# Alternating the order in which an FFN's float32r matmuls read their moving columns

## The chip, the cores and the metric

The kernel runs on one core of one Trainium2 chip. The metric is the device time of one execution in microseconds. Times are medians of several executions, and a profiled execution has a time of its own.

## What is computed

The input `x` has 4 x 1024 tokens of 512 features, all in float32. Two layers follow, each with a normalised input and a normalised output that is added to the residual:

```python
x = x + _layernorm(_L0_attn_ref(_layernorm(x), Wq, Wv, Wo, Wg, ln_gamma, ln_beta, beta))
x = x + _layernorm(_L0_ffn_ref(_layernorm(x), gate_w, up_w, down_w, gate_scale, up_scale, down_scale))
```

The first layer is a retention: `v = x @ Wv.T` is run through a decaying scan along the tokens, multiplied by `q = x @ Wq.T`, normalised, gated with `silu(x @ Wg.T)` and multiplied by `Wo.T`. The second layer, which the change touches, is a gated FFN with 1536 inner features, whose weights are rounded to an 8-bit floating point grid:

```python
wq = w.astype(jnp.float8_e4m3fn).astype(x.dtype)
gate = silu((x @ gate_wq) * gate_scale)
up = (x @ up_wq) * up_scale
out = ((gate * up) @ down_wq) * down_scale
```

## The kernel before

**Tiling.** The 4096 tokens are cut into 8 blocks of 512 (`TB`, `NB`). A block's features stand on 128 partitions in 4 chunks (`NC`), its tokens in 4 sub-blocks of 128 (`NS`), the inner features of the FFN in 12 chunks (`NI`). The loop over blocks (line 1250) and over the 12 inner chunks (line 1253) runs the FFN of block t, and between its steps it places by hand the steps of the retention of block t+1 and the input work of block t+2. The instructions of each engine are issued in the order in which the program writes them (`InOrder`, line 66, which is why the profile puts nearly all of them on line 74).

**Kinds of products.** The retention's products are plain float32 in the first four blocks; in blocks 2 and 3 they are built from half-size products of 256 columns (`product`, line 677). In the last four blocks q, v and g are float32r products of three parts, `top`, `low` and `diff` (`pass_of`, line 606), where `top` reads the normalised input `xnT` in runs of 32 columns, and `low` and `diff` read unbroken rows.

**The FFN.** All its products are float32r. The normalised input stands as an upper part and a rest in one tile, `x1nT` (line 945), so that a product is done twice, once for each part. For inner chunk i, `Ffn.gate` (line 988) and `Ffn.up` (line 994) call `project` (line 283), which makes 4 chunks x 2 parts = 8 matmuls of 128 x 128 stationary weights and 512 moving token columns into one PSUM bank of 512 columns, with start on the first and stop on the last. ScalarE applies silu and scale to gate, VectorE multiplies up by it (`fuse`, line 998), and the product is again split into an upper part (`act.copy`, line 1006) and a rest (`rest`, line 1009). `down` (line 1016) then uses this tile as the stationary operand, 128 token columns at a time, and a row of 512 columns of `down_sb` as the moving one: 4 sub-blocks x 2 parts = 8 matmuls, accumulated over the 12 chunks in four PSUM banks, `pds[0]` to `pds[3]`.

**The weights.** Gate, up and down weights come from DRAM in 18 pieces (line 116) of 1024 columns, in turn gate, up and down. VectorE and ScalarE round each to the 8-bit grid (`round_weights`, line 178). The last step of a piece is a subtraction that writes it into `gate_sb`, `up_sb` or `down_sb` (line 193). This lies in the first part of the kernel.

Of the kernel before, what the change touches and what calls it, by code (L numbers as in the profile page):

```python
# [15 lines left out]
ALU = mybir.AluOpType  # L16

P = 128
# [5 lines left out]
def retention_ffn_sandwich(  # L24
# [22 lines left out]
    NC = D // P  # L47
# [4 lines left out]
    Q = 32  # L52
# [13 lines left out]
    class InOrder:  # L66
# [9 lines left out]
    pe, dve, act, pool, sp = (  # L76
        InOrder(e) for e in (nc.tensor, nc.vector, nc.scalar, nc.gpsimd, nc.sync)
    )
# [30 lines left out]
    down_sb = wpool.tile([P, NI, D], F32R, tag="down_sb", name="down_sb")  # L109
    gate_v = gate_w.rearrange("(c p) f -> p c f", p=P)  # L110
    up_v = up_w.rearrange("(c p) f -> p c f", p=P)
    down_v = down_w.rearrange("(c p) f -> p c f", p=P)

    PW = 2 * NC * P
    pieces = []
    for h in range(NI // 2):
        pieces += [
            (gate_sb[:, :, ts(h, 2 * P)], gate_v[:, :, ts(h, 2 * P)]),
            (up_sb[:, :, ts(h, 2 * P)], up_v[:, :, ts(h, 2 * P)]),
            (down_sb[:, ts(h, 2), :], down_v[:, ts(h, 2), :]),  # L120
        ]


# [39 lines left out]
    parts = s0 + s1 + [s2]  # L163
# [6 lines left out]
    ]  # L170

    def as_dst(z, n):
        return z.rearrange("p (a b) -> p a b", a=pieces[n][0].shape[1])

    def load_piece(n):
        sp.dma_start(as_dst(parts[places[n][0]], n), pieces[n][1])

    def round_weights():

        def unit(n):
            w, c = (parts[k] for k in places[n])
            dve.tensor_scalar(c.bitcast(I32), w.bitcast(I32), 0x7F800000, None, ALU.bitwise_and)
            open_units.append((n, c))

        def finish(n):
            w, c = (parts[k] for k in places[n])
            if any(m == n for m, _ in open_units):
                units()  # L190
            dve.tensor_tensor(w, w, c, ALU.add)
            yield
            dve.tensor_tensor(pieces[n][0], as_dst(w, n), as_dst(c, n), ALU.subtract)
            for m in range(n + 1, len(pieces)):
                if freed_by[m] == n:
                    load_piece(m)
            yield

        unit(0)
        yield  # L200
        for n in range(len(pieces)):
            if n + 1 < len(pieces):
                unit(n + 1)
                yield
            yield from finish(n)
# [4 lines left out]
    def units():  # L210

        while open_units:
            _, c = open_units.pop(0)
            act.activation(c, c, AF.Relu, bias=neg_low)
            act.activation(c, c, AF.Identity, scale=1.5 * 2.0**20, bias=low_unit)
# [60 lines left out]
    def shift_scale(dst, src, mv):  # L276
# [3 lines left out]
        act.activation(nb, nb, AF.Identity, scale=mv[:, 1:2])  # L280
        act.activation(dst, src, AF.Identity, bias=nb, scale=mv[:, 1:2])

    def project(po, w, col, parts, tokens=slice(None)):


        out = po.rearrange("p (g j) -> p g j", j=Q) if len(parts[0].shape) == 4 else po
        for c in range(NC):
            for h, part in enumerate(parts):
                pe.matmul(
                    out[:, tokens], w[:, c, ts(col, P)], part[:, c, tokens],  # L290
                    start=(c == 0 and h == 0), stop=(c == NC - 1 and h == len(parts) - 1),
                )

# [197 lines left out]
    class Retention:  # L491
# [308 lines left out]
        def v(self, c, home="pa", tokens=slice(None)):  # L800
            if c not in self.pv:
                self.pv[c] = ps_tile(f"pv_{self.t}_{c}", home)
            project(self.pv[c], wv_sb, c, [self.by_chunk], tokens)
# [16 lines left out]
        def q(self, c, home="pa", tokens=slice(None)):  # L820
            if c not in self.pq:
                self.pq[c] = ps_tile(f"pq_{self.t}_{c}", home)
            project(self.pq[c], wq_sb, c, [self.by_chunk], tokens)
# [55 lines left out]
        def gate(self, c, home="pa"):  # L879
            self.pg[c] = ps_tile(f"pg_{self.t}_{c}", home)  # L880
            project(self.pg[c], wg_sb, c, [self.by_chunk])
# [91 lines left out]
    class Ffn:  # L973
# [42 lines left out]
        def down(self, i, tokens=None):  # L1016
            f = self.f[i]
            for s in range(NS) if tokens is None else tokens:
                for h in range(2):
                    pe.matmul(  # L1020
                        self.pds[s], f[:, h, ts(s, P)], down_sb[:, i, :],
                        start=(i == 0 and h == 0), stop=(i == NI - 1 and h == 1),
                    )

# [92 lines left out]
    a = Retention(0, x_first)  # L1117
# [20 lines left out]
    b = Retention(1)  # L1138
# [111 lines left out]
    for t in range(NB):  # L1250
        f, n = Ffn(a), None
        fast = b is not None and b.fast
        for i in range(NI):
            if t > 0 and (t > 1 or i) and not (fast and i == 11):
                (f if i else l).rest((i - 1) % NI)
            if t == 0 and i == 0:
                n = Retention(2)
# [314 lines left out]
            if b and i == 4 and 0 < t < NB - 2:  # L1572
                n = Retention(t + 2)
# [4 lines left out]
        l, a, b = f, b, n  # L1578
# [67 lines left out]
```

## Time and profile before

| what | value |
|---|---|
| median of 3 executions | 963.05 us (962.04 to 963.44) |
| the profiled execution | 961.99 us |
| its span in the trace | 960.2 us |
| FFN matmuls gate, up, down | 768 each |
| busy time of these, us | 194.9, 199.4, 192.0 |
| weight loads of each | 188 ns mean |

The busy time of down is the sum of its three groups in the profile, 183.6 us with the tile `fuse` and 8.4 and 4.0 us with the two tiles that hold it in the last block. A group is all instructions that read and write tiles of the same names in the same shape. A row of the timeline gives when a run of them starts, how long it lasts, the engine, the line, the tiles written and read, the tile sizes and the count. A matmul's duration reaches from its start to a modelled end and overlaps the next one's, so the time that a matmul takes from TensorE is read from the starts of successive ones. The profile prints f32 for both float32 and float32r operands of a matmul.

### The profile page before, as it was taken

The numbers are of one execution on the slowest core, as the hardware profiler recorded it, in microseconds if no ns is written. First come the engines' busy times: TensorE is split into PE (matmuls) and PEld (weight loads), VectorE is DVE, ScalarE is ACT, GpSimd is POOL, SyncE is SP. The second block draws the span as 40 slices with busy tenths as digits, with TensorE's granted clock in tenths as the row PEclk, the third lists the DMA queues.
The fourth block names the chain that finished last, engine by engine and source line by source line (L and its number), as shares of the span: only waits on it lengthen the run. The fifth ranks groups of instructions, "written<-read, shape, count | busy, mean of one in ns | idle before, by whom it ended". The sixth has DMA issues, their size and how long they took to land.

```text
span 960.2 us, 11914 instructions
## 1 busy us (share of the span) xinstructions
PE 944.8 (98%) x4022; PEld 744.4 (78%) x4022; DVE 670.0 (70%) x1042; ACT 441.4 (46%) x709; POOL 274.1 (29%) x340
## 2 busy tenths in 40 slices
PE   9999999999999999999999999999999999999997
PEld 7455766778888888887778887888878888788885
DVE  5996999677787877784776745866557855646445
ACT  3555675467666126352353525534264432625223
POOL 1404131412327033250432405232152502314020
PEclk9999999999999999999999999999999999999999
DMA  9411423864638757458655654556554465414021
GB/s 300 128 43 67 154 67 85 224 196 153 197 109 245 247 166 231 132 156 277 224 176 143 182 169 153 169 150 198 154 194 149 107 219 148 149 44 132 1 89 44
DMA packets 115756, 148.14 MB, mean 154 GB/s; under 512 B 10352, under 2 KB 61040, under 8 KB 115696
## 3 DMA queue, kind: packets, MB, share of 16 engines
q1 hardware_dynamic: 114832, 146.72, 49.9%
q8 instruction: 32, 0.52, 0.2%
q10 hardware_dynamic: 864, 0.66, 0.2%
q14 instruction: 28, 0.23, 0.1%
HBM read 108.81 MB, written 42.47 MB: 158 GB/s over the span
## 4 chain that ended last, share of the span: by engine, by line
PE 73%; DVE 10%; ACT 4%; POOL 4%; DMA 4%; issue 3%; SPq 1%; DVEq 0%; ACTq 0%; POOLq 0%
PE pfg L74 14%; PE pfu L74 14%; PE pd L74 12%; PE po L74 9%; PE pv L74 9%; PE pq L74 8%; PE pg L74 7%; DVE st L74 2%; DVE y L74 1%; SPq L74 1%; POOL d L74 1%; DVE scr L74 1%; DMA w_ring_parts<-dlow_v 1%; DVE fuse L74 1%; DVE gate L74 1%
## 5 line engine op out<-in xcount | busy, mean ns | idle before, releaser
L74 PE MATMUL pfu<-x1nT,up_sb 128*128 128x512 f32 x768 | 199.4, 402 | 0.0
L74 PE MATMUL pfg<-x1nT,gate_sb 128*128 128x512 f32 x768 | 194.9, 395 | 0.2
L74 PE MATMUL pd<-down_sb,fuse 128*128 128x512 f32 x720 | 183.6, 397 | 0.0
L74 PEld LDWEIGHTS pfu<-x1nT,up_sb 128*128 128x128 f32 x768 | 144.3, 188 | 32.5 <-issue 3.1
L74 PEld LDWEIGHTS pfg<-x1nT,gate_sb 128*128 128x128 f32 x768 | 144.1, 188 | 30.6 <-DVE x1nT L74 1.0
L74 PEld LDWEIGHTS pd<-down_sb,fuse 128*128 128x128 f32 x720 | 135.2, 188 | 27.8
L74 ACT CAST fuse<-gate 128x512 fp32r<-128x512 f32 x90 | 55.6, 617 | 160.1 <-DVE gate L74 160.0
L74 ACT ACTIVATE gate<-pfg,gs_sb 128x512 f32<-128x512 f32 x96 | 65.7, 684 | 108.2 <-PE pfg L74 108.1
L74 DVE SCALAR_TENSOR_TENSOR gate<-pfu,us_sb,gate 128x512 f32<-128x512 f32 x96 | 71.5, 745 | 54.3 <-PE pfu L74 51.3
L74 POOL TENSOR_SCALAR mv<-mv 128x1 f32<-128x1 f32 (+1 forms) x82 | 24.0, 292 | 249.5 <-DVE mv L74 246.3
L74 DVE TENSOR_TENSOR fuse<-gate,fuse 128x512 fp32r<-128x512 f32 x90 | 75.7, 841 | 5.5 <-ACT fuse L74 5.5
L74 DVE BATCH_NORM_STATS2 st<-x 128x6 f32<-128x512 f32 x64 | 43.7, 683 | 21.4 <-POOL x L74 18.8
L74 POOL TENSOR_TENSOR mv<-mv,nhalf 128x1 f32<-128x1 f32 (+1 forms) x75 | 53.6, 715 | 6.2
L74 POOL TENSOR_TENSOR ysum<-y 128x512 f32<-128x512 f32 (+1 forms) x10 | 12.0, 1202 | 149.6 <-DVE y L74 149.5
L74 DVE TENSOR_TENSOR mids<-po,mids 128x512 f32<-128x512 f32 x30 | 20.5, 684 | 41.2 <-PE po L74 40.9
L74 POOL TENSOR_TENSOR x<-x,x1n 128x512 f32<-128x512 f32 x32 | 41.5, 1298 | 14.9 <-ACT x1n L74 14.9
L74 POOL TENSOR_TENSOR d<-d,x 128x512 f32<-128x512 f32 x28 | 36.0, 1310 | 18.3 <-ACT d L74 16.5
L74 POOL TENSOR_TENSOR sqsum<-sqsum,sq 128x512 f32<-128x512 f32 x24 | 35.0, 1457 | 14.8 <-ACT sq L74 13.2
L74 POOL TENSOR_TENSOR ysum<-ysum,y 128x512 f32<-128x512 f32 (+1 forms) x20 | 22.2, 1111 | 47.3 <-DVE y L74 46.9
L74 DVE RECIPROCAL rstd<-rstd 128x512 f32<-128x512 f32 x8 | 26.8, 3351 | 11.9 <-ACT rstd L74 11.9
L74 DVE TENSOR_TENSOR y<-pq,y 128x512 f32<-128x512 f32 x18 | 12.4, 690 | 31.2 <-PE pq L74 31.2
L74 ACT ACTIVATE scr<-scr,neg_low 128x1024 f32<-128x1024 f32 x18 | 20.6, 1145 | 24.1 <-DVE scr L74 24.0
(201 smaller groups left out, 1625.5 us busy)
## 6 DMA issues: line engine op xcount, KB each, us to landing
kept<-x SPq DMA_DIRECT2D x32, 256.0 KB, 2.7
x<-kept SPq DMA_DIRECT2D x32, 256.0 KB, 4.5
x<-in_x SPq DMA_DIRECT2D x28, 256.0 KB, 4.3
out<-d SPq DMA_DIRECT2D x27, 256.0 KB, 2.0
mx<-xs SPq DMA_DIRECT2D x18, 256.0 KB, 2.1
xnT<-mx SPq DMA_DIRECT2D x32, 128.0 KB, 4.2
w_ring_parts<-dtop_v SPq DMA_DIRECT2D x16, 256.0 KB, 3.5
w_ring_parts<-dlow_v SPq DMA_DIRECT2D x16, 256.0 KB, 3.0
```

The source lines that it names most:

```text
L74: return lambda *args, **kwargs: tc.keep_in_program_order(op(*args, **kwargs))
```

## The change

No instruction is added or removed. What changes is in which order operands are read and written.

- Gate and up: the moving row of 512 token columns is read as two halves in turn, column 0, 256, 1, 257 and so on. The bank is written in consecutive order, so position 2u + k of it holds token 256k + u. Silu, multiplication and splitting work on this order as they did on the other.
- Down, stationary: the tile `fuse` now holds the tokens in that order, so the 128 tokens of a sub-block are every second column of it.
- Down, moving: `down_sb` holds the even columns of a row in its first half and the odd ones in the second. The matmul reads the two halves in turn, so the bank gets the columns in their natural order, and all that follows is as before.
- The subtraction that writes a piece into `down_sb` writes it in this split order.

The branches for three-dimensional rows and banks in the new functions are not reached by any call: only `project` with two parts and `down` use them, with two-dimensional ones.

```diff
-            (down_sb[:, ts(h, 2), :], down_v[:, ts(h, 2), :]),
+            (
+                down_sb[:, ts(h, 2), :].rearrange("p a (k u) -> p a u k", k=2),
+                down_v[:, ts(h, 2), :],
+            ),
...
     def as_dst(z, n):
-        return z.rearrange("p (a b) -> p a b", a=pieces[n][0].shape[1])
+        return z.rearrange("p (a b) -> p a b", a=2 if n % 3 == 2 else NC)
+
+    def like(z, n):
+        z = as_dst(z, n)
+        return z.rearrange("p a (u k) -> p a u k", k=2) if n % 3 == 2 else z
...
-            dve.tensor_tensor(pieces[n][0], as_dst(w, n), as_dst(c, n), ALU.subtract)
+            dve.tensor_tensor(pieces[n][0], like(w, n), like(c, n), ALU.subtract)
...
+    def in_turn(row):
+
+        if len(row.shape) == 3:
+            return row.rearrange("p (k g) j -> p g j k", k=2)
+        return row.rearrange("p (k u) -> p u k", k=2)
+
+    def as_read(bank):
+
+        if len(bank.shape) == 3:
+            return bank.rearrange("p (g j) k -> p g j k", j=Q)
+        return bank.rearrange("p (u k) -> p u k", k=2)
+
+    def in_order(bank):
+
+        return bank.rearrange("p (u k) -> p k u", k=2)
+
     def project(po, w, col, parts, tokens=slice(None)):
...
+                to, row = out[:, tokens], part[:, c, tokens]
+                if len(parts) > 1:
+                    to, row = as_read(to), in_turn(row)
                 pe.matmul(
-                    out[:, tokens], w[:, c, ts(col, P)], part[:, c, tokens],
+                    to, w[:, c, ts(col, P)], row,
                     start=(c == 0 and h == 0), stop=(c == NC - 1 and h == len(parts) - 1),
                 )
...
                     pe.matmul(
-                        self.pds[s], f[:, h, ts(s, P)], down_sb[:, i, :],
+                        as_read(self.pds[s]), in_order(f[:, h, :])[:, s // 2, ts(s % 2, P)],
+                        down_sb[:, i, :].rearrange("p (k u) -> p u k", k=2),
                         start=(i == 0 and h == 0), stop=(i == NI - 1 and h == 1),
                     )
```

## The prediction

> **What bounds the kernel now.** I read the busy shares first, then the slices, then TensorE's waits, then the timeline of TensorE for the time from one matmul's start to the next.
>
> ```profile
> PE 944.8 (98%) x4022; PEld 744.4 (78%) x4022; DVE 670.0 (70%) x1042; ACT 441.4 (46%) x709; POOL 274.1 (29%) x340
> ...
> PE   9999999999999999999999999999999999999997
> ...
> PEclk9999999999999999999999999999999999999999
> ```
>
> TensorE is busy in every slice and at its full clock. Busy alone would not prove it the bound, because the ends of matmuls are modelled. So I looked at TensorE's waits: eleven entries, 7.9 us together (the longest is 1.4). The span is 960.2 us, so nothing makes TensorE wait for long, and its time is the sum of what its matmuls take one after another. That sum is read from starts. First a stretch near the end where only the FFN runs (start, then duration, then the group):
>
> ```profile
> 893.14 1.98 PE L74 MATMUL pfu<-x1nT,up_sb 128*128 128x512 f32 x8
> 894.95 1.98 PE L74 MATMUL pfg<-x1nT,gate_sb 128*128 128x512 f32 x8
> ...
> 905.83 1.98 PE L74 MATMUL pd<-down_sb,fuse 128*128 128x512 f32 x8
> 907.64 1.98 PE L74 MATMUL pfg<-x1nT,gate_sb 128*128 128x512 f32 x8
> 909.46 1.98 PE L74 MATMUL pfu<-x1nT,up_sb 128*128 128x512 f32 x8
> 911.27 1.07 PE L74 MATMUL pd<-down_sb,fuse 128*128 128x512 f32 x4
> ```
>
> From 893.14 to 911.27 lie ten groups of eight: 18.13/80 = 226.6 ns from start to start, the same for gate, up and down. These are the float32r products (the profile prints f32 for both kinds). Next the plain float32 products:
>
> ```profile
> 70.38 13.90 PE L74 MATMUL po<-wo_sb,y 128*128 128x512 f32 x32
> ...
> 340.70 1.89 PE L74 MATMUL pq<-t_sums,w_ring 128*128 128x256 f32 x8
> 342.24 2.18 PE L74 MATMUL pfu<-x1nT,up_sb 128*128 128x512 f32 x8
> 344.25 1.89 PE L74 MATMUL pq<-t_sums,w_ring 128*128 128x256 f32 x8
> ```
>
> The 32 of 512 columns take 13.90 us, the last one's 0.59 included (their mean duration is 592 ns): 13.31/31 = 429 ns each. From 340.70 to 344.25 lie eight float32 of 256 columns and eight float32r: 3.55 - 8 x 0.2266 = 1.74, or 217 ns each. [...] Something costs each float32r product about 10.5 ns. Last, the float32r products outside the FFN:
>
> ```profile
> 608.68 1.11 PE L74 MATMUL pg<-xnT,w_ring_parts 128*128 128x512 f32 x4
> 609.63 1.07 PE L74 MATMUL pg<-low,w_ring_parts 128*128 128x512 f32 x4
> 610.54 1.75 PE L74 MATMUL pfg<-x1nT,gate_sb 128*128 128x512 f32 x7
> ```
>
> The four that read `low`, an unbroken row, take 0.91/4 = 227 ns. The four that read `xnT` in sixteen runs of 32 columns take 0.95/4 = 237.5 ns: fifteen jumps cost about 10 ns, 0.67 each. The float32 products that read the same `xnT` pay no such sum: from 142.40 to 147.66 us the trace has eight of those and eight float32r, 5.26 us, so (5.26 - 1.81)/8 = 431 ns each, 2 more than the unbroken 429. [...]
>
> [...]
>
> **The change part by part.** It adds and removes no instruction and no wait; the order of work on each engine is as before.
>
> Reading order: the FFN has 8 blocks x 12 x (8 gate + 8 up + 8 down) = 2304 products, 2304 x 226.6 = 522 us of the 960. If each half of a row is served on its own, [...] the slot falls to the floor: 226.6 - 215.8 = 10.8 ns, times 2304 = 24.9 us. All of it lies on the path, since TensorE has next to no waits. If the jumps cost what they cost in `xnT`, the bound on the other side is far above (rival below). I take the floor, and say why: [...] the price of a jump is measured only between long runs of a single stream.
>
> Stationary columns of down with a step of two: 768 loads, 188 ns each now, beside the matmul before (slot 226.6). [...] I take 0. [...] A gain from this part I exclude, because the load is hidden already.
>
> Writing `down_sb` in two halves: six VectorE subtractions of 1024 elements, 1.23 us each (one 2.17) between 33 and 161 us. The data and count are the same; I take 0. If the writes were twice as slow, 6 x 1.2 = 7 us of VectorE, of which only what delays TensorE counts: VectorE is at 33.84 of 35.00 us in the window 95 to 130 and 37.41 of 42.00 after, so at most some 3 us would show. The same full VectorE bounds the gain: the first block's FFN, 288 products or 3.1 us of gain, runs beside it, and I take off 1 us for what VectorE gives back there.
>
> What is late next: in the remaining blocks VectorE is at 55 to 79 per cent in the windows I read, and the weights from DRAM made TensorE wait 1.5 us in all. A TensorE that is 5 per cent faster in half of its time still waits for nothing long.
>
> Sum, against the profiled execution: 961.99 - 24.9 + 1 = 938.1 us (961.99 is its span of 960.2 and 1.8 around it). The median of the runs shown is 963.05, 1.06 above, so 939.1. The median can tell from no change only what exceeds about 0.2%, or 2 us.
>
> **The rivals.** *Only part of the excess goes* (some fixed cost of a float32r product remains, or a start-up): half of it gives 12.5 us, 950.6. For it: nothing shows that all 10.8 ns scale with the read. [...]
>
> *Nothing changes*: the excess isn't in the order of reading but in the kind of product; 963. Against: the runs of `xnT` move it.
>
> *Each change of place stalls the read* (the other side). Place: the moving read of all 2304 products. Price: 0.67 ns, as between the runs of `xnT`, at each of the 255 returns to the first half: 171 ns, so 398 ns a product, 2304 x 171 = +394 us, 1357. It decides very early: the gain of 10.8 ns is spent at 10.8/255 = 0.04 ns a return. For it: [...] the jumps of `xnT`. Against: the two streams take turns[...].
>
> *The loads of down lose their cover*: gate and up win 1536 x 10.8 = 16.6 us[...].
>
> **How the numbers follow.** The floor reached (939): 0.60. Part of it (945 to 960): 0.15. Unchanged: 0.05. Stalls at each turn (1357): 0.16. Loads of down exposed (999): 0.04. Faster 0.75, same 0.05, slower 0.20. The range holds the first three: from 935 (nothing given back, and some of the slots of 230 to 236 ns that stand among the 227 ones gone too) to 965. The slow cases lie far away and are left out, 0.20. Most of the chance is on one side, so no second range is needed.
>
> **What would show it.** In the timeline of the changed kernel's end, ten groups of eight FFN products should take 17.3 us instead of 18.13 (216 ns a slot), and `low` and `xnT` stay at 227 and 237. If gate and up are at 216 and down is not, the stationary step is to blame. If slots are near 400, the turns stall. If slots are at 216 and the time isn't down by over 20 us, a wait on VectorE has taken TensorE's place. The six subtractions into `down_sb` should stay near 1.23 us. The forecast is wrong if two interleaved streams are not served apart.

## The result and the profile after

The changed kernel takes 948.62 us (median of 4, 946.70 to 949.78) where the kernel before takes 962.96 beside it: a ratio of 0.985, 95% interval 0.9831 to 0.9869, or 14.3 us less. The profiled execution took 946.70 us, with a span of 944.9; that is 15.3 us less than before, and the sums below are made against this pair.

The page of the changed kernel, busy shares and slices:

```profile
PE 922.8 (98%) x4022; PEld 752.8 (80%) x4022; DVE 673.4 (71%) x1042; ACT 440.1 (47%) x709; POOL 273.2 (29%) x340
...
PE   9999999999999999999999999999999999999996
...
PEclk9999999999999999999999999999999999999999
```

TensorE is busy as before, with the same number of instructions. But the page also has the chain of work that ended last, followed back from the end, as shares of the span. Before and after:

```profile
PE 73%; DVE 10%; ACT 4%; POOL 4%; DMA 4%; issue 3%; SPq 1%; DVEq 0%; ACTq 0%; POOLq 0%
PE 64%; DVE 20%; ACT 5%; POOL 3%; DMA 3%; issue 2%; SPq 2%; DVEq 0%; POOLq 0%; ACTq 0%
```

VectorE's share has doubled. In the stretch from 24 to 200 us, where the weights are rounded, the chain was 53 per cent TensorE and 27 per cent VectorE; now it is 10 and 60. TensorE's timeline in the stretch near the end where the FFN runs alone:

```profile
878.71 1.89 PE L74 MATMUL pfg<-x1nT,gate_sb 128*128 128x512 f32 x8
880.44 1.89 PE L74 MATMUL pfu<-x1nT,up_sb 128*128 128x512 f32 x8
...
892.53 1.89 PE L74 MATMUL pd<-down_sb,fuse 128*128 128x512 f32 x8
...
897.71 1.89 PE L74 MATMUL pd<-down_sb,fuse 128*128 128x512 f32 x8
```

From 878.71 to 897.71 lie eleven groups of eight: 19.00/88 = 215.9 ns from start to start, where it was 226.6. Gate, up and down are all at the slot forecast. Its 215.8 ns was the author's estimate. The trace of before has float32 products of 256 columns beside it, at 215.5 on average (112 slots of `po<-w_ring_parts,t_sums`). Then products that the change doesn't touch, further ahead in the timeline, first before and then after:

```profile
605.97 1.07 PE L74 MATMUL pg<-diff,w_ring_parts 128*128 128x512 f32 x4
606.87 1.98 PE L74 MATMUL pd<-down_sb,fuse 128*128 128x512 f32 x8
...
598.17 1.89 PE L74 MATMUL pfu<-x1nT,up_sb 128*128 128x512 f32 x8
599.90 1.09 PE L74 MATMUL pg<-diff,w_ring_parts 128*128 128x512 f32 x4
600.83 1.89 PE L74 MATMUL pd<-down_sb,fuse 128*128 128x512 f32 x8
```

The four of `diff`, which stand right behind a group of the FFN, take 0.93/4 = 232.5 ns; before they took 0.90 us, or 225. And TensorE's waits (us in total, times, longest), four of the eleven before and then the longest after:

```profile
PE pt L74 <- DVE x1n L74: 1.2, 1, 1.2
PE var L74 <- DVE half L74: 0.9, 4, 0.3
PE pv L74 <- DMA w_ring_parts<-dlow_v: 0.8, 2, 0.5
PE po L74 <- DVE mids L74: 0.4, 1, 0.4
...
PE pfu L74 <- DVE gate L74: 2.5, 2, 2.2
PE pt L74 <- DVE x1n L74: 1.8, 1, 1.8
PE var L74 <- DVE half L74: 1.7, 4, 0.4
PE po L74 <- DVE mids L74: 1.4, 1, 1.4
PE mu L74 <- DVE half L74: 1.4, 3, 1.0
PE pv L74 <- ACT xnT L74: 1.4, 2, 1.2
PE pq L74 <- ACT pq L74: 1.4, 1, 1.4
```

All twelve entries come to 14.3 us, against 7.9 before. The largest is new. The waits on VectorE rose from 3.5 to 9.8 us and those on ScalarE from 1.9 to 3.7, while those on weights from DRAM fell from 2.0 to 0.4. The six writes of `down_sb` are longer too (nanoseconds min/median/max, then the first and last start); first four of them before, then all six after:

```profile
L74 DVE TENSOR_TENSOR down_sb<-scr x4: 1224/1226/2171, 33.2 to 160.5; 128x1024 fp32r<-128x1024 f32 x4
...
L74 DVE TENSOR_TENSOR down_sb<-scr x4: 1968/2004/2915, 32.7 to 161.4; 128x1024 fp32r<-128x1024 f32 x4
L74 DVE TENSOR_TENSOR down_sb<-scr,scr x2: 1999/2006/2012, 98.8 to 139.5; 128x1024 fp32r<-128x1024 f32 x2
```

So I kept an account. A slot is the mean from start to start within groups, with starts over 300 ns apart left out. Both kernels run the same 4022 matmuls in the same order, so the time from each start to the next can be set beside its counterpart; the last column adds up these differences.

| what | before | after | change in the span |
|---|---|---|---|
| gate and up, 1536 slots | 227.7 ns | 215.85 ns | -18.3 us |
| down, 768 slots | 227.2 ns | 215.8 ns | -8.9 us |
| `xnT`, `low`, `diff`, 192 slots each | 236.4, 227.35, 226.9 ns | 239.0, 228.7, 233.1 ns | +1.6 us |
| all other products | | | +2.3 us |
| starts with a wait listed in either kernel, taken out of the rows above | 7.9 us of waits | 14.3 us of waits | +7.7 us |
| after the last matmul's start | | | +0.3 us |
| span | 960.2 us | 944.9 us | -15.3 us |

The time won in the FFN's slots is even a little more than forecast, 27.2 us. Some 12 us of it come back. The row of all other products is mainly lateness, not slower slots: 17 starts that are 0.09 to 0.43 us late make up 2.0 of its 2.3 us. Such delays are partly or wholly missing from the list of waits, since a wait counts only from the modelled end of the product before, which lies some 160 ns after the next start in a dense stream (duration 379, slot 216).

The same comparison shows where. Taking 10.8 ns for each product of the FFN as due, 4.4 us of the gain due so far are gone by the 700th matmul (200 us before the change): it starts 1.4 us later than it did before. By the 1800th (447 us) 6.6 are gone, and from there to the end another 2.7. (Ahead of the prediction, the busy time of down stands as 192.0 us; its three groups add up to 196.0. Nothing here rests on it.)

### The profile page after: what moved, and what is told of

The parts are those of the page before. It is cut to its first block, busy times and chain, and to the rows that moved or that the text cites. A ratio compares the mean times of both kernels' runs of the same rounds, so it can differ in the third digit from the quotient of the medians.

```text
span 944.9 us, 11926 instructions
## 1 busy us (share of the span) xinstructions
PE 922.8 (98%) x4022; PEld 752.8 (80%) x4022; DVE 673.4 (71%) x1042; ACT 440.1 (47%) x709; POOL 273.2 (29%) x340
## 4 chain that ended last, share of the span: by engine, by line
PE 64%; DVE 20%; ACT 5%; POOL 3%; DMA 3%; issue 2%; SPq 2%; DVEq 0%; POOLq 0%; ACTq 0%
PE pfu L74 12%; PE pfg L74 12%; PE pd L74 11%; PE pv L74 8%; PE pq L74 7%; PE po L74 7%; PE pg L74 5%; DVE y L74 4%; DVE scr L74 3%; DVE st L74 2%; SPq L74 2%; DVE gate L74 1%; POOL mv L74 1%; DVE fuse L74 1%; DVE down_sb L74 1%
## 5 line engine op out<-in xcount | busy, mean ns | idle before, releaser
L74 PE MATMUL pfu<-x1nT,up_sb 128*128 128x512 f32 x768 | 189.8, 390 | 2.5 <-DVE gate L74 2.5
L74 PE MATMUL pfg<-x1nT,gate_sb 128*128 128x512 f32 x768 | 185.9, 384 | 0.2
L74 PE MATMUL pd<-down_sb,fuse 128*128 128x512 f32 x720 | 175.3, 386 | 0.0
L74 PEld LDWEIGHTS pd<-down_sb,fuse 128*128 128x128 f32 x720 | 141.3, 196 | 15.2
```

Of the source, the lines that this page charges most:

```text
L74: return lambda *args, **kwargs: tc.keep_in_program_order(op(*args, **kwargs))
```

## The experiments

Two questions were open. What in the order of reading saves the 10.8 ns? And what gives back the rest: the slower subtractions (theory A), a VectorE and ScalarE that are full in the first blocks anyway (theory B), or TensorE's own slots?

### Orders of reading by themselves

```python
run("row", seq)                      # room[:, i % 4, :]
for d in (256, 128, 64, 32, 16, 8, 4, 2):
    run(f"apart{d}", fold(d), ...)   # "p (a k u) -> p a u k", k=2, u=d
run("quarters", ...); run("tworows", ...); run("evens", ...); run("step4", ...); run("runs32", ...)
run("statstep2", seq, ...); run("turnstatstep2", fold(256), ...)
run("stat64", seq, ...); run("stat32", seq, ...)
...                                  # 256 and 384 columns, one tile again and again, float32
```

> This kernel leaves out the whole computation: it copies 512 rows of x to the output again and again, and runs series of 32 matmuls with a 128x128 stationary tile each and 512 moving columns in different orders, each series into PSUM in consecutive order. From start to start: theory 1 (a stall each time a single stream moves on in the row, hidden when two streams take turns) expects 227 ns for an unbroken row, 216 for two halves in turn (256 columns apart), 216 also at smaller distances down to some unit of the memory, 227 again below it, about 237 for runs of 32, and the same 227 with a stationary tile of 64 or 32 columns. Theory 2 (the moving read collides with the load of the next stationary tile, and the turn changes only when they meet) expects the excess over 216 to shrink with the stationary tile: 221 with 64 columns, 219 with 32. Theory 3 (a fixed cost of each float32r product that the order happens to remove) expects the same 10.8 ns of excess with 256 or 384 columns; theory 1 expects half and three quarters of it.

Timeline of this kernel (digits at the end of names are left out, so the eight distances stand in one row):

```profile
22.43 7.42 PE L75 MATMUL t_row<-room,stat 128*128 128x512 f32 x32
29.69 55.80 PE L75 MATMUL t_apart<-room,stat 128*128 128x512 f32 x256
85.33 9.20 PE L75 MATMUL t_quarters<-room,stat 128*128 128x512 f32 x32
94.36 7.07 PE L75 MATMUL t_tworows<-room,stat 128*128 128x512 f32 x32
101.27 14.60 PE L75 MATMUL t_evens<-room,stat 128*128 128x512 f32 x32
115.69 14.94 PE L75 MATMUL t_step<-wide,stat 128*128 128x512 f32 x32
130.45 7.76 PE L75 MATMUL t_runs<-room,stat 128*128 128x512 f32 x32
...
145.30 7.63 PE L75 MATMUL t_statstep<-room,stat 128*128 128x512 f32 x32
152.77 7.07 PE L75 MATMUL t_turnstatstep<-room,stat 128*128 128x512 f32 x32
159.68 14.90 PE L75 MATMUL t_stat<-room,stat 128*64 128x512 f32 x64
...
201.96 13.89 PE L75 MATMUL t_plain<-raw 128*128 128x512 f32 x32
215.69 17.44 PE L75 MATMUL t_plainturn<-raw 128*128 128x512 f32 x32
```

The difference of two starts, divided by 32, gives the slot. Unbroken row: (29.69 - 22.43)/32 = 227 ns. Two separate rows in turn: (101.27 - 94.36)/32 = 216. Runs of 32: 237. A window on the end of the row of distances splits it:

```profile
77.82 7.67 PE L75 MATMUL t_apart<-room,stat 128*128 128x512 f32 x33
```

Up to 77.82 lie 223 products, 48.13/223 = 215.8 ns, so the distances from 256 columns down to 4 all stand there. The last 32, at 2 columns (8 bytes), take (85.33 - 77.82 - 0.22)/32 = 228. So reading in turn pays with 4 columns (16 bytes) between the two streams and does not with 2. No order of 512 columns measured here is faster than 215.8 ns. What is slow is every second column (8-byte step, 451 ns), every fourth (461), and four streams in turn (282).

Theory 2 falls: with a stationary tile of 64 and then 32 columns the unbroken row takes (174.41 - 159.68)/64 = 230 ns, not less. Using the same stationary tile or the same moving row again and again leaves it at 227 to 228. The lengths do not settle theories 1 and 3: 256 columns took 120 ns unbroken and 111.5 in turn, an excess of 8.4 where theory 1 expects 5.4 and theory 3 10.8. 384 columns took 175 unbroken, but had no series in turn beside them. And float32 products in turn got worse, 540 ns for 429, so of the two kinds only float32r gains. (Each float32 product stands in the trace as two matmuls, 32 for the 16 of this series; the times here and in the prediction are those of one of the two.)

### The subtraction with unbroken writes

```diff
-                down_sb[:, ts(h, 2), :].rearrange("p a (k u) -> p a u k", k=2),
+                down_sb[:, ts(h, 2), :].rearrange("p a (k u) -> p a k u", k=2),
...
-        return z.rearrange("p a (u k) -> p a u k", k=2) if n % 3 == 2 else z
+        return z.rearrange("p a (u k) -> p a k u", k=2) if n % 3 == 2 else z
```

> The subtraction into down_sb runs over the halves in the outer loop, so it writes unbroken rows and reads every second column (8 bytes apart) in place of writing alternately into two halves. Theory A (most of what was given back in the first two blocks comes from these six subtractions, 2.0 us each in place of 1.23) expects them back near 1.23 us and the time 2 to 4 us below that of the change, 945 to 946.5. Theory B (VectorE is full there anyway, and a faster TensorE only waits for it) expects the subtractions shorter but the time within 1 us of the change, 948 to 949. If the strided read costs as much as the alternate write, neither is tested.

```profile
L74 DVE TENSOR_TENSOR down_sb<-scr x4: 1224/1226/2174, 33.4 to 160.8; 128x1024 fp32r<-128x1024 f32 x4
L74 DVE TENSOR_TENSOR down_sb<-scr,scr x2: 1550/1570/1591, 99.6 to 139.2; 128x1024 fp32r<-128x1024 f32 x2
```

Four subtractions are back at their old time, and two nearly. The time is 947.44 us (ratio 0.9837, 0.9814 to 0.9861): 1.2 us under the change, within both intervals. Against the starts of before, only 0.7 us is given back at the 600th matmul, where the change had given back 1.3. At the 900th it is 3.3 where the change had 4.6. By the end of the profiled executions that lead is lost, with 3.0 us of waits on weights from DRAM where the change had 0.4. So 4 us less VectorE work hardly move the end, and theory A carries little.

### Only gate and up, only down

Gate and up alone keep down's moving row and `down_sb` as they were (shown against the kernel before; the parts of gate and up are those of the change):

```diff
...
-                        self.pds[s], f[:, h, ts(s, P)], down_sb[:, i, :],
+                        self.pds[s], in_order(f[:, h, :])[:, s // 2, ts(s % 2, P)],
+                        down_sb[:, i, :],
```

> Gate and up read their halves in turn and down takes every second stationary column, but down_sb is in natural order and read as an unbroken row. Gate and up should stand at 216 ns a product and gain 1536 x 10.8 = 16.6 us. Theory A: no slow subtraction, so about 3 of it are given back to waits on VectorE, 949 to 950. Theory B: some 5 to 6 given back, 952. If the strided stationary load costs something, down's products stand above 227 ns.

It took 954.48 us (0.9906, 0.9876 to 0.9936), worse than all expected. Gate and up have 215.8 ns slots. But down has 232.8 instead of 227.2, which costs 768 x 5.6 = 4.3 us: an unbroken product pays when the stationary tile beside it is loaded from every second column. The bench shows the same without any other engine, (152.77 - 145.30)/32 = 233. In turn, with the same strided load, it is (159.68 - 152.77)/32 = 216. So it is down's own reading in turn that keeps its slot at 216 beside strided loads.

Down alone leaves gate and up, and the stationary columns, as before (shown against the change):

```diff
-                if len(parts) > 1:
-                    to, row = as_read(to), in_turn(row)
...
-                        as_read(self.pds[s]), in_order(f[:, h, :])[:, s // 2, ts(s % 2, P)],
+                        as_read(self.pds[s]), f[:, h, ts(s, P)],
```

> Only down reads its moving row in turn, with down_sb in split order; gate and up read unbroken rows and the stationary columns are unbroken. Down should stand at 216 ns, gate and up at 227: 768 x 10.8 = 8.3 us. Theory A: the six slow subtractions give back about 4, so 958 to 959. Theory B: TensorE is hardly faster in the first two blocks, so only 1 to 2 are given back, 956.

It took 960.39 us (0.9975, 0.9966 to 0.9984): 2.5 of the 8.3 us. Down stands at 215.9, gate and up at 228.3, 0.6 ns more than before. TensorE's waits rose to 11.4 us, among them 1.6 for the transpose of `x1n` and 1.3 for `gate`, both on VectorE. In the account for this run the slots of down give 8.9 us, 3.7 come back at starts with a listed wait and 2.9 in the other rows; 0.3 more lie after the last start. Both theories missed the size. The two parts alone, 8.5 and 2.5 us, come to 11 where together they give 14.3. They are worth more together, mainly since gate and up alone leave down's unbroken rows beside strided loads, which costs 4.3 us.

### The first blocks with VectorE and ScalarE relieved

```diff
-            dve.tensor_scalar(c.bitcast(I32), w.bitcast(I32), 0x7F800000, None, ALU.bitwise_and)
-            open_units.append((n, c))
+            pass
...
-            dve.tensor_tensor(w, w, c, ALU.add)
...
-            dve.tensor_tensor(pieces[n][0], like(w, n), like(c, n), ALU.subtract)
+            dve.tensor_tensor(pieces[n][0], like(w, n), like(w, n), ALU.max)
```

This is the edit of the changed kernel; the kernel before gets the same, with its own order of writing. The changed kernel keeps its six slow writes of `down_sb` (2.0 us each).

> The kernel before with the rounding of the FFN's weights left out: of the three VectorE and two ScalarE steps for each of the 18 pieces only the last write stays, so VectorE has about 39 us less to do in the first two blocks and ScalarE 41. It is the base for the next run. Both theories expect it a few us below the kernel before (TensorE waits little there): 955 to 962.

961.17 us (0.9989, 0.998 to 0.9997): the old kernel barely notices the relief.

> The changed kernel with the same rounding left out. Theory B (what is given back in the first blocks is TensorE running into a full VectorE and ScalarE) expects it 19 to 22 us below the run before_lean, because only the float32r products outside the FFN and later waits still give something back. The rival (the slots of TensorE themselves, not other engines, give it back) expects the difference to stay at 14 to 15.

943.51 us (0.9812, 0.9793 to 0.9831): 17.7 us below its base, where the full pair has 14.3. So the same relief is worth 1.5 us to the old kernel and some 5 to the new one. That is theory B's direction, short of the size it expected: about 3 us of what was given back is TensorE running into the rounding work. The intervals leave this figure uncertain by some 2.7 us, but the traces point the same way. Between 24 and 200 us the chain that ended last is 76 per cent TensorE in both kernels without rounding, and at the 900th matmul 1.5 us are given back between these two where the full pair had 4.6. TensorE's waits went to 10.5 us (7.0 in the old kernel without rounding):

```profile
PE po L74 <- DVE mids L74: 1.7, 2, 1.2
PE var L74 <- DVE half L74: 1.6, 4, 0.4
PE pv L74 <- DMA w_ring_parts<-dlow_v: 1.6, 4, 0.7
```

The wait for `gate` is gone and that for the `x1n` of the transpose is down to 0.2; those for `mids`, `half` and the weights of the later blocks stay.

### Mixed orders by themselves, and all float32r products in turn

> This kernel leaves out the whole computation, as the other bench. Series in which eight products of one order are followed by four of another, eight times over: unbroken then unbroken, in turn then unbroken, in turn with every second stationary column then unbroken, in turn then in turn; then runs of 32 columns, alone and with their two halves in turn. If an unbroken product pays more just after products read in turn, the four unbroken ones stand at 230 to 235 ns in the second and third series against 227 in the first. If the rise of diff in the changed kernel comes from other engines' use of the memory, they stand at 227 in all three. Runs of 32 should be 237 alone and 216 in turn.

```profile
24.00 1.07 PE L96 MATMUL rr_then<-room,stat 128*128 128x512 f32 x4
24.90 1.98 PE L96 MATMUL rr_first<-room,stat 128*128 128x512 f32 x8
...
43.94 1.89 PE L96 MATMUL tr_first<-room,stat 128*128 128x512 f32 x8
45.67 1.09 PE L96 MATMUL tr_then<-room,stat 128*128 128x512 f32 x4
46.60 1.89 PE L96 MATMUL tr_first<-room,stat 128*128 128x512 f32 x8
...
107.12 7.75 PE L96 MATMUL ru_first<-room,stat 128*128 128x512 f32 x32
114.70 7.07 PE L96 MATMUL ri_first<-room,stat 128*128 128x512 f32 x32
```

Four unbroken products take 0.90 us behind unbroken ones and 0.93 behind products in turn. Product by product these are 238, 232, 231 and 227 ns, so it takes a few products to settle. (In the trace of the changed kernel, the four of `diff` behind a group of gate take 236.7, 232.2, 230.5 and 227.9 on average.) With every second stationary column it is 232 on average too. No other engine computes in these series, and all eight rounds of the second, from 43.94 to 65.17 us, show the same 0.92 to 0.93 us. So the same rise of `diff` in the changed kernel needs no other engine: it is TensorE's own. Runs of 32 in turn stand at 216.

That points to a version that reads the other 576 float32r products in turn as well. It starts from the run with unbroken writes of `down_sb`; of its edit, the reading of v and g is left out here:

```diff
...
-            out_ = bank.rearrange("p (g j) -> p g j", j=Q) if part == "top" else bank
+            out_ = as_read(bank)
+            if part == "top":
+                out_ = as_read(out_)
...
-                    out_, w[:, i, :], x[:, i], start=part == "top" and i == 0, stop=True,
+                    out_, w[:, i, :], in_turn(x[:, i]), start=part == "top" and i == 0, stop=True,
...
-                dve.tensor_tensor(y[:, c, :], bank, y[:, c, :], ALU.mult)
+                dve.tensor_tensor(by_half(y[:, c, :]), in_order(bank), by_half(y[:, c, :]), ALU.mult)
...
```

> The changed kernel with the subtraction that writes unbroken rows, and with the 576 float32r products of top, low and diff read in two halves in turn as well; the banks of v, q and g then hold tokens in turn and VectorE and ScalarE read every second column of them (the scan of v as two scans of 256 columns). If the turn costs nothing at group borders, all of these products fall to 216: 384 x 10.8 + 192 x 21.4 = 8.3 us, and another 2 us come from the unbroken products that now stand at 230 to 240 behind an FFN group: 937 to 939. Rival: strided reads of the banks slow VectorE down and half of it goes: 942 to 944.

941.58 us (0.9784, 0.9769 to 0.9799), 21.1 us below the kernel before, 7.0 below the change and 5.9 below the run with unbroken writes.

```profile
594.27 1.03 PE L74 MATMUL pg<-xnT,w_ring_parts 128*128 128x512 f32 x4
595.13 1.03 PE L74 MATMUL pg<-low,w_ring_parts 128*128 128x512 f32 x4
596.00 1.89 PE L74 MATMUL pfu<-x1nT,up_sb 128*128 128x512 f32 x8
597.72 1.03 PE L74 MATMUL pg<-diff,w_ring_parts 128*128 128x512 f32 x4
598.59 1.89 PE L74 MATMUL pd<-down_sb,fuse 128*128 128x512 f32 x8
```

Each four take 0.86 to 0.87 us, 216 ns. It falls between the two expectations. Against the run with unbroken writes the slots of the 576 products save 9.7 us, close to the 10.3 expected, but TensorE's waits are now 17.9 us, with 3.1 for one kind of weight transfer. In these runs, the less time TensorE's own products take, the more of its waits come out: 7.9 us in the span of 960.2 before, 11.4 in 958.1 with down alone, 11.6 in 952.5 with gate and up alone, 14.3 in 944.9 with the change (15.1 in 945.7 with unbroken writes) and 17.9 in 939.5 here.

## Why the prediction was right, and where it was not

**What bounds the kernel** was right for the kernel before, TensorE by the sum of its slots, with less to spare than was read: in the first blocks a quarter of the chain was VectorE already.

**Reading order** was right to the nanosecond where the FFN runs alone, 226.6 to 215.9. No series of 512 columns in these runs went clearly below 215.8. The mechanism was not shown. The prediction's "each half of a row is served on its own" was the author's assumption. It fits two streams in turn at 215.8 ns from 256 columns apart down to 4, but at 2 columns apart they take 228, and four streams in turn take 282. Nor are float32 products a model of it: they pay next to nothing for the runs of `xnT` (431 ns for 429), yet get slower in turn (540). Why a single unbroken stream takes 10.8 ns more is not settled, nor why four streams are slow. A cost per jump of a single stream, the rival's reading of `xnT` (0.67 ns a jump, 398 ns a product), did not carry over to turns, which took 215.9.

**Part of the excess, nothing changes, stalls, exposed loads**: none happened. The loads of down did become longer (196 ns for 188) and stayed hidden, at 215.8 ns a slot, but only because the product beside them is read in turn: unbroken it took 232.8 beside such loads. The 999 us named for exposed loads was the author's estimate, which no run shows.

**Writing `down_sb`**, taken as 0, was 0.78 us more for each of the six, within the bound of twice as slow. Writing unbroken instead won 1.2 us, which lies within the intervals.

**What is late next** is the step that failed in size: "still waits for nothing long", and 1 us taken off. The waits on VectorE and ScalarE more than doubled, from 5.4 to 13.5 us, while those on weights, which the prediction looked at, fell. VectorE was busy for 153 of the 176 us from 24 to 200 and still is for 155, but now the chain runs through it. About 3 us of what came back depend on the rounding work there. In the later blocks VectorE's busy share, 55 to 79 per cent, was read as slack, yet single results (`half`, `mids`) made TensorE wait 0.9 and 0.4 us before and 3.1 and 1.4 afterwards.

**"`low` and `xnT` stay at 227 and 237"** was wrong by 1.3 and 2.6 ns within groups, and `diff` by 6.2: 1.6 us that no part of the sum held.

So 939.1 was forecast and 948.62 measured: the term for the gain stands, 27.2 us for 24.9, and the term for what is given back is some 12 us instead of 1. The range held the result by its breadth. 948.62 lies where the prediction had put "part of it", at a chance of 0.15, though the cause named there did not occur: the excess went wholly. What did occur is one of its signs, slots at 216 and a time not down by 20 us, with VectorE on the chain in the first blocks.

## What to carry to other kernels

Where float32r products bound a kernel, compare their slot with that of a float32 matmul of half the columns in the same trace (here 226.6 and 215.5 ns); whether the order of reading removes the difference is worth testing with a bench of a few series. Change all such products together: a product in the old order paid more here beside one in the new (`diff` 233.1 ns for 226.9). And when the bound engine is to get 3 per cent faster, don't read slack from busy shares, but ask for each result that it takes from another engine how long before its use it was ready.

## What was unexpected of the hardware

- Two streams only 16 bytes apart, in turn, are enough for 215.8 ns; 8 bytes apart they take 228. One stream with an 8-byte step takes 451, about twice the 227 of the unbroken row.
- Float32 matmuls, for which 256 columns took 215.5 to 217 ns in the trace of before, become slower in turn: 429 to 540 ns with 512 columns.
- An unbroken float32r product needs several like it before it to settle at 227 (238, 232, 231, 227), and stands at 233 beside a stationary load of every second column.
- On VectorE, writing alternately into two halves of a row took 2.0 us for 1024 columns; reading every second one and writing unbroken took 1.23 to 1.57.
